# The second attention's gates on VectorE instead of GpSimd, and the last two outputs in place

## The chip, the cores and the metric

The kernel runs on one core of one Trainium2 chip. A core has five engines that work side by side: TensorE (PE) multiplies matrices into PSUM, VectorE (DVE) and ScalarE (ACT) work elementwise on SBUF and PSUM, GpSimd (POOL) works elementwise on SBUF, and SyncE (SP) issues DMAs here. The metric is the time of one execution on the device, in microseconds (us), lower being better.

## What is computed

The reference has two layers over x of 4 × 1024 tokens of width 128, all in fp32:

```python
xn = _layernorm(x)
s = _L0_attn_ref(xn, ...)            # 16 heads, window of 64 tokens, ALiBi
g = _silu(_L0_ffn_ref(xn, ...))      # 8 experts mixed into one weight per batch
x = x + s * g
xn = _layernorm(x)
s = _L1_attn_ref(xn, ...)            # below
g = _silu(_L1_ffn_ref(xn, ...))      # gated, then two square layers of 512, then back to 128
x = x + s * g
```

The second attention takes the first axis (4) as its sequence: each of the 1024 positions attends over its own 4 batch entries, with 16 heads of 8 elements. The part that the change touches is its gate on the position bias:

```python
g = jax.nn.sigmoid(g.reshape(B, H, T, 2, 4).sum(-1))
gate_a = g[..., 0:1]
gate_b = g[..., 1:2]
gate_a_1 = gate_a * (gate_b * grep_a - 1.0) + 2.0
attn = attn + gate_a_1 * position_bias[None]
probs = jax.nn.softmax(attn, axis=-1)
```

The kernel writes a sigmoid as 0.5 + 0.5 · tanh(half), so the gate becomes (tanh_a + 1) · (tanh_b · 0.25 · grep_a + 0.25 · grep_a − 0.5) + 2.

## The kernel before

**Stages.** x, xn and the second layer's gate g1 lie in SBUF as 128 partitions × 4 batches × 1024 tokens. The first layer and the second layer's feed-forward run over eight units of half a batch (512 tokens); the second attention runs over eight slices of 128 positions, each with all four batches. As the second attention of a slice needs nothing but its own 128 columns of the four batches, it starts while the first layer still runs (from about 340 us) and ends with the kernel. Slices 0 to 3 need the first halves of the batches, slices 4 to 7 (`late`) the second halves.

**Order.** ORDER is a list written out by hand. Each word is one step, and the steps emit their instructions engine by engine in just that order; each engine runs its own instructions in order, so an instruction that waits holds up all behind it on its engine. Words with a star belong to the second attention: for slice n, `*An` projects one batch (four times), `*Bn` takes the gates' tanh, `*bn` forms the products, `*Cn` the scores, `*En` the exponentials, `*Nn` the normalisation, `*Dn` the values (twice, two batch entries each), `*Gn` their total, `*Tn` turns back, `*Fn` projects out, `*Yn` writes the slice's output. `wn`, `hn`, `in` and `jn` are the quarters of unit n's feed-forward: the gated pair (two matrices of 128×512), the two square layers, and the way back. The list ends:

```python
*C6 h7 *E6 *F1 *A7 *B7 h7 *Y4 *F5 h7 *N6 *b7 *Y1 *C7 h7 *E7 *D6 *Y5 *N7 *T2 i7 *F2 *D7 *D6 *D7 *G6 i7
*Y2 i7 *F0 *T6 *G7 *F3 *F6 *Y3 *T7 *Y6 i7 *F7 j7 *Y0 *Y7 j7 y0 y1
```

**The steps that matter here.** `attend` holds the second attention. `products` (`*b`) multiplies each query by each key on VectorE (L631) and then, on GpSimd, forms the gate ga from the tanh values in six operations (L640 to L646), the last of which, gb, multiplies it with the position bias for all 4 × 4 pairs. `score` (`*C`) sums the products over a head's elements (L658, L660), adds gb (L661) and takes the maximum off (L664, L665). `norm` (L674 to L676) and `values` (L682 on VectorE, L689 on GpSimd) follow, `total` is L694. `gated_out` (`*Y`) adds the bias out of PSUM (L715), multiplies with g1 (L716), adds x on GpSimd (L717) and starts a DMA (L718).

For late slices `gated_out` writes only batches 0 to 2. The last batch's second half waits for the feed-forward of the last unit (`j7`, L590 on TensorE and L593 on ScalarE, in two halves), and is written by `last_batch` (`y0`, `y1`) in two pieces of 256 columns: xn times g1 (L732), plus x (L733), and a DMA (L734). Both `gated_out` and `last_batch` take a buffer `t2k` for it, of which there are three in rotation; so a step can't write its buffer before the DMA of the step three buffers earlier has read it.

**Banks.** PSUM banks are taken in the order of the table BANKS, one digit a request, from three banks M0 to M2: a request waits until the last reader of that bank's earlier content is done. In the feed-forward's gated pair the second bank of a pair is read by L569 on VectorE, the first by L568 on ScalarE; the square layers' banks are read by L578 on ScalarE, the projections' by L620 and L621.

Of the kernel before, what the change touches and what calls it, by code (L numbers as in the profile page):

```python
# [12 lines left out]
ALU = mybir.AluOpType  # L13
# [3 lines left out]
P = 128  # L17
B, S, D = 4, 1024, 128
H, HD = 16, 8
# [20 lines left out]
G = 2 * H  # L40
# [6 lines left out]
def constants():  # L47
# [67 lines left out]
BANKS = (  # L115
    "0120120120102102102102102121021012012012021021020120120120120201201201201201021012010210210212102102"
    "1021020120121210210210210210212121010201201212012021021021021210210210210210210210210210210201021021"
    "010210210210210210210210210210210210210210120120120120120120120101201202101012"
)


# [1 line left out]
def block_kernel(ctx: ExitStack, tc: tile.TileContext, a: dict, out: bass.AP):  # L123
    nc = tc.nc
    PE, DVE, ACT, POOL = nc.tensor, nc.vector, nc.scalar, nc.gpsimd
# [14 lines left out]
    def t2k():  # L140
        return tmp.tile([P, 512], F32, tag="t2k", name="t2k", bufs=3)
# [7 lines left out]
    g1 = main.tile([P, B, S], F32, tag="g1", name="g1")  # L149
# [12 lines left out]
    qga = const.tile([P, 2, H], F32, tag="qga", name="qga")  # L162
# [13 lines left out]
    def v(name, i=0, n=1):  # L176
        at = VEC[name][0] + i
        return vec[:, at:at + n]
# [5 lines left out]
    xn = main.tile([P, B, S], F32, tag="xn", name="xn")  # L184
# [103 lines left out]
    def program(exact):  # L288
# [8 lines left out]
        def big(shape=(P, 4, 4, P)):  # L297
            return ffn.tile(list(shape), F32, tag="big", name="big", bufs=6)
# [298 lines left out]
        def attend(sl, pool, late):  # L597
# [30 lines left out]
            def products():  # L628
                pd = st["pd"] = big((P, B, B, D))
                m = st["qkg"]  # L630
                DVE.tensor_tensor(  # L631
                    pd,
                    m[:, :, 0:D].unsqueeze(2).to_broadcast([P, B, B, D]),
                    m[:, :, D:2 * D].unsqueeze(1).to_broadcast([P, B, B, D]),
                    ALU.mult,
                )

                gate = st["gate"]
                ga = pool.tile([P, B, H], F32, tag="ga", name="ga")
                POOL.tensor_tensor(ga, gate[:, :, H:G], qga[:, 0:1, :].to_broadcast([P, B, H]), ALU.mult)  # L640
                POOL.tensor_tensor(ga, ga, qga[:, 1:2, :].to_broadcast([P, B, H]), ALU.add)
                POOL.tensor_scalar(gate[:, :, 0:H], gate[:, :, 0:H], 1.0, None, ALU.add)
                POOL.tensor_tensor(ga, ga, gate[:, :, 0:H], ALU.mult)
                POOL.tensor_scalar(ga, ga, 2.0, None, ALU.add)
                gb = st["gb"] = pool.tile([P, B, B, H], F32, tag="gb", name="gb")
                POOL.tensor_tensor(  # L646
                    gb,
                    ga.unsqueeze(2).to_broadcast([P, B, B, H]),
                    v("pb", 0, B * B * H).rearrange("p (t s h) -> p t s h", t=B, s=B),
                    ALU.mult,  # L650
                )
# [56 lines left out]
            def gated_out():  # L708
# [10 lines left out]

            steps_of = {  # L720
                "B": gates, "b": products, "C": score, "E": power, "N": norm, "G": total, "T": turn_back, "F": project_out, "Y": gated_out,
            }
            for letter, parts_of in (("A", project), ("D", values)):
# [3 lines left out]
        def last_batch(i):  # L727

            n = U // 2
            y = t2k()[:, 0:n]  # L730
            r = slice(U + i * n, U + i * n + n)
            DVE.tensor_tensor(y, xn[:, B - 1, r], g1[:, B - 1, r], ALU.mult)  # L732
            DVE.tensor_tensor(y, y, x[:, B - 1, r], ALU.add)  # L733
            nc.sync.dma_start(out=out[:, (B - 1) * S + r.start:(B - 1) * S + r.stop], in_=y)  # L734

# [103 lines left out]
        def scaled_w3():  # L839
# [10 lines left out]
            "z": second_gates, "Z": scaled_w3,  # L850
            "L": lambda i: load(*(("w1", "w2", "h1"), ("h2", "w3"), ("wa", "x"))[i]), "0": lambda n: idle(cst, P * n), 
            "y": last_batch,
            **{"*" + c: slices(c) for c in "ABbCENDGTFY"},
        }
        banks["next"] = iter(BANKS[BEGIN:])
        for word in ORDER.split():
            n = 2 if word[0] == "*" else 1
# [78 lines left out]
```

## Time and profile before

| | |
|---|---|
| median of 3 runs | 540.52 us (540.14 to 540.78) |
| the profiled execution | 540.1 us, of which the span 538.3 us |
| TensorE's granted clock | 0.99 of full speed over the span |
| the gates on GpSimd, L640 to L646, 8 times each | 4.2, 7.8, 7.5, 5.4, 4.4 and 8.4 us busy |
| VectorE's L661 idle before it for gb | 3.0 us in 4 places |
| products, L631, 128×2048 | 2.30 us each, 8 times |
| last two L732 and L733 | 0.47 and 0.42 us each |

How much each engine has to do in the stretches of the second attention (start and end, length, and busy time of PE, PEld, DVE, ACT and POOL, then clock, DMA share and GB/s):

```profile
340.00:375.00 35.00, 35.00 (x360) 18.20 (x360) 22.41 (x31) 28.16 (x36) 7.55 (x14) 1.00 0.01 1
395.00:420.00 25.00, 24.91 (x202) 13.19 (x205) 19.56 (x27) 18.82 (x22) 7.13 (x8) 1.00 0.01 2
440.00:475.00 35.00, 34.90 (x88) 15.87 (x87) 29.18 (x43) 23.78 (x34) 16.09 (x16) 1.00 0.00 0
475.00:490.00 15.00, 15.00 (x77) 10.32 (x76) 12.29 (x21) 8.85 (x16) 6.46 (x6) 1.00 0.00 1
490.00:530.00 40.00, 39.13 (x157) 22.57 (x156) 36.89 (x48) 17.65 (x25) 25.91 (x23) 1.00 0.12 36
```

TensorE is busy in all of them. VectorE is busy 22.4 of 35 us at the beginning of the second attention, and 36.9 of 40 at its end. A number before a line's bracket in later views is idle time of that engine ahead of the instruction, with what ended it. Numbers of lines are those of the kernel before.

### The profile page before, as it was taken

The numbers are of one execution on the slowest core, as the hardware profiler recorded it, in microseconds if no ns is written. First come the engines' busy times: TensorE is split into PE (matmuls) and PEld (weight loads), VectorE is DVE, ScalarE is ACT, GpSimd is POOL, SyncE is SP. The second block draws the span as 40 slices with busy tenths as digits, with TensorE's granted clock in tenths as the row PEclk, the third lists the DMA queues.
The fourth block names the chain that finished last, engine by engine and source line by source line (L and its number), as shares of the span: only waits on it lengthen the run. The fifth ranks groups of instructions, "written<-read, shape, count | busy, mean of one in ns | idle before, by whom it ended". The sixth has DMA issues, their size and how long they took to land.

```text
span 538.3 us, 10515 instructions
## 1 busy us (share of the span) xinstructions
PE 520.2 (97%) x4448; PEld 293.6 (55%) x4448; DVE 348.5 (65%) x657; ACT 369.1 (69%) x436; POOL 124.2 (23%) x149
## 2 busy tenths in 40 slices
PE   8599999999999999999999999999999999999994
PEld 4267554475465645555555674554564564455463
DVE  6899885466465443415745554665778577988993
ACT  3678673797859676694999637887995655765432
POOL 4013230110011010000020020211613253725762
PEclk9899999999999999999999999999999999999998
DMA  8925021110240011021301000000000000000103
GB/s 315 414 80 197 3 75 44 40 62 20 81 154 3 2 40 39 2 79 39 118 2 40 1 1 1 2 2 0 1 1 2 1 0 1 0 1 2 35 24 105
DMA packets 10727, 27.33 MB, mean 51 GB/s; under 512 B 1040, under 2 KB 5296, under 8 KB 9648
## 3 DMA queue, kind: packets, MB, share of 16 engines
q1 hardware_dynamic: 10240, 25.01, 13.3%
q10 hardware_dynamic: 432, 1.57, 0.8%
q8 instruction: 37, 0.61, 0.5%
q14 instruction: 18, 0.15, 0.1%
HBM read 24.48 MB, written 2.10 MB: 49 GB/s over the span
## 4 chain that ended last, share of the span: by engine, by line
PE 77%; DVE 12%; POOL 3%; ACT 3%; issue 2%; DMA 1%; DVEq 0%; POOLq 0%; ACTq 0%
PE ps_M L577 32%; PE ps_S L426 6%; PE ps_O L474 5%; PE ps_M L517 5%; PE ps_M L590 5%; PE ps_M L528 4%; PE ps_M L565 4%; PE ps_M L566 4%; PE ps_M L619 3%; DVE big L682 2%; DVE big L443 2%; PE ps_M L232 1%; DMA out<-t2k 1%; PE ps_M L273 1%; ACT big L777 1%
## 5 line engine op out<-in xcount | busy, mean ns | idle before, releaser
L577 PE MATMUL ps_M<-big,l1h 128*128 128x512 f32 x512 | 229.3, 595 | 0.9 <-ACT big L578 0.5
L577 PEld LDWEIGHTS ps_M<-big,l1h 128*128 128x128 f32 x512 | 94.9, 190 | 111.8 <-issue 105.9
L443 DVE TENSOR_TENSOR big<-ps_S,bias 128x2048 f32<-128x2048 f32 x32 | 73.2, 2287 | 32.4 <-PE ps_S L426 26.4
L578 ACT ACTIVATE big<-ps_M,vec 128x512 f32<-128x512 f32 x64 | 43.7, 687 | 60.5 <-PE ps_M L577 60.2
L777 ACT ACTIVATE big<-big 128x2048 f32<-128x2048 f32 x32 | 60.9, 1910 | 9.1 <-DVE big L443 8.8
L578 ACT ACT_TABLE_LOAD x41 | 52.6, 1283 | 7.6 <-PE ps_M L577 6.9
L538 POOL TENSOR_TENSOR g<-g,s 128x512 f32<-128x512 f32 x8 | 10.2, 1273 | 200.1 <-DVE s L508 130.7
L569 DVE SCALAR_TENSOR_TENSOR big<-ps_M,vec,t2k 128x512 f32<-128x512 f32 x32 | 24.0, 749 | 36.3 <-PE ps_M L566 19.9
L426 PE MATMUL ps_S<-qm,k 32*64 32x256 f32 (+1 forms) x768 | 37.4, 472 | 4.5 <-DVE big L443 4.3
L474 PEld LDWEIGHTS ps_O<-big,vb 128*32 128x32 f32 x2048 | 30.3, 112 | 11.1 <-issue 8.0
L568 ACT ACTIVATE t2k<-ps_M,vec 128x512 f32<-128x512 f32 x32 | 22.0, 686 | 19.4 <-PE ps_M L565 19.2
L474 PE MATMUL ps_O<-big,vb 128*32 128x64 f32 x2048 | 33.4, 223 | 1.0 <-issue 0.6
L565 PE MATMUL ps_M<-xn,l1w 128*128 128x512 f32 x64 | 33.4, 603 | 0.2
L566 PE MATMUL ps_M<-xn,l1w 128*128 128x512 f32 x64 | 32.8, 594 | 0.8 <-ACT t2k L568 0.8
L517 PE MATMUL ps_M<-xn,mw 128*128 128x512 f32 x64 | 33.3, 609 | 0.0
L528 PEld LDWEIGHTS ps_M<-mw,big 128*128 128x128 f32 x256 | 30.1, 192 | 4.1 <-issue 3.0
L590 PEld LDWEIGHTS ps_M<-l1w,big 128*128 128x128 f32 x256 | 30.2, 192 | 4.0 <-issue 3.6
L352 DVE SCALAR_TENSOR_TENSOR mw<-tw,gr,mw 128x512 f32<-128x512 f32 x42 | 31.1, 746 | 0.5
L528 PE MATMUL ps_M<-mw,big 128*128 128x128 f32 x256 | 31.1, 276 | 0.0
L590 PE MATMUL ps_M<-l1w,big 128*128 128x128 f32 x256 | 30.9, 276 | 0.0
L214 POOL TENSOR_SCALAR rstd<-mv 128x4 f32<-128x4 f32 x16 | 8.4, 527 | 97.3 <-DVE mv L212 90.8
L689 POOL TENSOR_TENSOR big<-big 128x512 f32<-128x512 f32 x16 | 22.2, 1387 | 34.5 <-DVE big L682 34.5
(164 smaller groups left out, 734.7 us busy)
## 6 DMA issues: line engine op xcount, KB each, us to landing
tw<-in_tw SPq DMA_DIRECT2D x24, 512.0 KB, 4.0
big<-in_tw SPq DMA_DIRECT2D x4, 1024.0 KB, 9.2
l1h<-in_l1h SPq DMA_DIRECT2D x2, 1024.0 KB, 8.6
bias<-in_bias ACTq DMA_DIRECT2D x1, 1024.0 KB, 8.7
x<-in_x SPq DMA_DIRECT2D x1, 1024.0 KB, 5.2
out<-t2k SPq DMA_DIRECT2D x4, 256.0 KB, 2.9
l1w<-in_l1w SPq DMA_DIRECT2D x3, 256.0 KB, 9.8
out<-t2k SPq DMA_DIRECT2D x4, 192.0 KB, 2.2
```

The source lines that it names most:

```text
L352: DVE.scalar_tensor_tensor(m, more[e // 2][:, e % 2, :], gr[:, e:e + 1], base if e == 0 else m, ALU.mult, ALU.add)
L426: PE.matmul(sp[rows, j, :, q0:q0 + n], lhsT=k[r, key:key + W], rhs=qm[r, :, t * P + q0:t * P + q0 + n], start=True, stop=True,)
L443: DVE.tensor_tensor(pr, sp, bias, ALU.add)
L474: PE.matmul(op[32 * j:32 * j + 32, part, qs], lhsT=vb[:, col:col + 32], rhs=pr[:, j, g, qs], start=(odd + i + g == 0), stop=(odd + i + g = ...
L517: PE.matmul(hp, lhsT=m1[:, c * P:(c + 1) * P], rhs=xn[:, b, cx], start=True, stop=True)
L528: PE.matmul(op[:, i, :], lhsT=hid[:, c, i * P:(i + 1) * P], rhs=m2[:, c * D:(c + 1) * D], start=(c + i == 0), stop=(c + i == FC + 2))
L565: PE.matmul(p1, lhsT=wt["w1"][:, c * P:(c + 1) * P], rhs=xn[:, b, cx], start=True, stop=True)
L566: PE.matmul(p2, lhsT=wt["w2"][:, c * P:(c + 1) * P], rhs=xn[:, b, cx], start=True, stop=True)
L577: PE.matmul(hp, lhsT=wt[name][:, i, c * P:(c + 1) * P], rhs=hid[:, i, :], start=(i == 0), stop=(i == FC - 1))
L578: ACT.activation(new[:, c, :], hp, AF.Gelu, scale=v(name + "s", c))
L590: PE.matmul(op[:, k, :], lhsT=hid[:, i, at0:at0 + P], rhs=wt["w3"][:, i, :], start=(i + k == 0), stop=(i + k == FC + n - 2))
L777: ACT.activation(pr, pr, AF.Exp)
```

## The change

The six operations of the gates move from GpSimd to VectorE; two of them, adding 1 to tanh_a and multiplying it in, become one fused operation, which leaves the tile `gate` as it was. They stay at their place in the program, after the products of the same slice. The two pieces of `last_batch` write into xn itself instead of a `t2k` buffer, and are sent from there. In BANKS eleven of the last twelve digits are others: from `*T2` on the requests take other ones of the three banks (`*F2` alone keeps M1).

```diff
-    "010210210210210210210210210210210210210210210120120120120120120120101201202101012"
+    "010210210210210210210210210210210210210210210120120120120120120120101021020212120"
...
                 gate = st["gate"]
                 ga = pool.tile([P, B, H], F32, tag="ga", name="ga")
-                POOL.tensor_tensor(ga, gate[:, :, H:G], qga[:, 0:1, :].to_broadcast([P, B, H]), ALU.mult)
-                POOL.tensor_tensor(ga, ga, qga[:, 1:2, :].to_broadcast([P, B, H]), ALU.add)
-                POOL.tensor_scalar(gate[:, :, 0:H], gate[:, :, 0:H], 1.0, None, ALU.add)
-                POOL.tensor_tensor(ga, ga, gate[:, :, 0:H], ALU.mult)
-                POOL.tensor_scalar(ga, ga, 2.0, None, ALU.add)
+                DVE.tensor_tensor(ga, gate[:, :, H:G], qga[:, 0:1, :].to_broadcast([P, B, H]), ALU.mult)
+                DVE.tensor_tensor(ga, ga, qga[:, 1:2, :].to_broadcast([P, B, H]), ALU.add)
+                DVE.scalar_tensor_tensor(ga, gate[:, :, 0:H], 1.0, ga, ALU.add, ALU.mult)
                 gb = st["gb"] = pool.tile([P, B, B, H], F32, tag="gb", name="gb")
-                POOL.tensor_tensor(
+                DVE.tensor_scalar(ga, ga, 2.0, None, ALU.add)
+                DVE.tensor_tensor(
                     gb,
                     ga.unsqueeze(2).to_broadcast([P, B, B, H]),
                     v("pb", 0, B * B * H).rearrange("p (t s h) -> p t s h", t=B, s=B),
...
             n = U // 2
-            y = t2k()[:, 0:n]
             r = slice(U + i * n, U + i * n + n)
-            DVE.tensor_tensor(y, xn[:, B - 1, r], g1[:, B - 1, r], ALU.mult)
+            y = xn[:, B - 1, r]
+            DVE.tensor_tensor(y, y, g1[:, B - 1, r], ALU.mult)
             DVE.tensor_tensor(y, y, x[:, B - 1, r], ALU.add)
             nc.sync.dma_start(out=out[:, (B - 1) * S + r.start:(B - 1) * S + r.stop], in_=y)
```

More of the change, by code (lines that the diff above doesn't have):

```diff
@@ L117 @@
     "1021020120121210210210210210212121010201201212012021021021021210210210210210210210210210210201021021"
-    "010210210210210210210210210210210210210210120120120120120120120101201202101012"
+    "010210210210210210210210210210210210210210120120120120120120120101021020212120"
 )
```

## The prediction

> **What bounds the kernel now.** I read four views in this order: the page's busy times and chain, the chain from 390 us on, the timeline around the places where that chain leaves TensorE, and the groups of instructions with shapes kept apart, for prices. First the page:
>
> ```profile
> PE 520.2 (97%) x4448; PEld 293.6 (55%) x4448; DVE 348.5 (65%) x657; ACT 369.1 (69%) x436; POOL 124.2 (23%) x149
> PE 77%; DVE 12%; POOL 3%; ACT 3%; issue 2%; DMA 1%; DVEq 0%; POOLq 0%; ACTq 0%
> ```
>
> TensorE has work nearly throughout, so a change elsewhere counts only where TensorE waits for it, or after its last instruction. The 23% left to others sit mostly in the second half. The chain from 390 us on (start, length, engine, tile, line) shows where:
>
> ```profile
> 457.68 2.46 POOL gate L642
> 463.09 0.44 DVE vb L661
> 465.25 2.21 DVE big L631
> 473.67 0.75 DVE big L569
> 474.47 1.13 PE ps_M L565 x2
> ...
> 494.05 0.86 POOL gb L646
> 494.94 0.43 DVE vb L661
> ...
> 499.63 2.32 DVE big L631
> ...
> 528.76 4.38 DMA out<-t2k
> 533.14 0.03 issue
> ```
>
> From 457.6 to 474.4 the chain is VectorE with GpSimd's gates inside it, and ends in a TensorE that waits for L569. From 489 to 523 it is VectorE almost without a gap, and at the end the last output waits for a DMA of the output two before it. The timeline of these places says how much slack there is (start, length; idle before and its releaser in brackets):
>
> ```profile
> 463.09 0.43 DVE L661 TENSOR_TENSOR vb<-vb,gb 128x256 f32<-128x256 f32 x1 [0.54 <-POOL gb L646]
> 474.47 0.30 PEld L565 LDWEIGHTS ps_M<-xn,l1w 128*128 128x128 f32 x2 [0.93 <-DVE big L569]
> ...
> 531.47 0.38 ACT L593 ACTIVATE g<-ps_M 128x256 f32<-128x256 f32 x1 [1.40 <-PE ps_M L590]
> 533.26 0.43 DVE L732 TENSOR_TENSOR t2k<-xn,g 128x256 f32<-128x256 f32 x1 [2.14 <-DMA out<-t2k]
> ```
>
> VectorE stops for the gates only where a slice's products and their sums are shorter than GpSimd's six operations; it waits 3.0 us in all, in four places (1.40, 0.54, 0.54, 0.54). TensorE at 474.47 starts 0.06 after L569's end: any delay of VectorE arrives there whole.
>
> [...] L642 on GpSimd takes 0.37 us alone and 2.48 beside the 2.28 us of L631, and L658 of a slice takes 1.94 us alone (at 353.97) but 2.27 at 467.48 where a gate operation holds it. [...]
>
> **The change part by part.** Prices from the groups by shape:
>
> ```profile
> L508 DVE TENSOR_TENSOR s<-ps_M,inv 128x64 f32<-128x64 f32 x16 | 3.4, 215 | 0.0
> L332 DVE TENSOR_TENSOR shares<-tb,gr 128x32 f32<-128x32 f32 x4 | 0.7, 186 | 0.1
> L661 DVE TENSOR_TENSOR vb<-vb,gb 128x256 f32<-128x256 f32 x4 | 1.7, 426 | 1.3 <-POOL gb L646 1.1
> L327 DVE SCALAR_TENSOR_TENSOR gr<-ps_M,vec 128x8 f32<-128x8 f32 x4 | 0.6, 161 | 1.2 <-PE ps_M L325 1.1
> L835 DVE TENSOR_SCALAR wa<-wa 128x128 f32<-128x128 f32 x1 | 0.2, 217 | 0.0
> ```
>
> Added per slice: two tensor_tensor of 64 elements, 0.22 each (between L332 and L661, and L508's 0.215); one fused operation of 64, 0.23 (L327's 0.161 at 8 elements, L352's 0.746 at 512); one tensor_scalar of 64, 0.19 (below L835's 128); gb, 0.43. Sum 1.29, plus 0.03 between dependent VectorE instructions (L664 ends at 464.13, L665 starts at 464.16) five times: 1.44 us. Eight slices: 11.5 us. Bounds: 1.25 (0.19 for each small one, no gaps) and 1.7 (0.25 each and gb at 0.55). Removed: GpSimd's 37.7 us (4.2+7.8+7.5+5.4+4.4+8.4). None is itself TensorE's wait; its worth is the four stops and the collisions.
>
> Instructions behind the new ones on VectorE are those behind L631 in each slice. Their order, and that of every other engine and of the DMA queue, is unchanged. New is only that VectorE itself now waits for the gate's tanh (L626); in all eight slices that ends before or within 0.2 us of L631, so this costs nothing.
>
> - Slices 0 to 3 (344 to 440 us). In slice 0, L443 starts 1.7 us later (347.7) and delays ScalarE's copies; ScalarE still has 0.35 us before L578 at 357.03 and 0.41 before L518 at 360.01. Of its 0.76 us about 0.3 reach TensorE at 361.0. In slice 1 VectorE is 1.44 late, but ScalarE idles 2.00 before L578 at 369.78 and VectorE 2.26 at 372.50. In slice 2, 1.44 replaces a wait of 1.40: nothing. In slice 3, VectorE waits 1.24 for GpSimd's rstd just behind the gates; what is left is gone at the 1.26 of idle time before L674 (441.59). Together +0.3 (bounds 0 and 0.8).
> - Slices 4 and 5. +1.44 − 0.54 = +0.90; then +1.44 − 0.32 (L658 at 2.27 back to 1.95) − 0.08 (the gap before L661) = +1.04. L569 ends 1.94 later and TensorE starts 1.94 later at 474.47; no TensorE idle time follows until 496 in which to regain it. With slices 0 to 3: +2.24.
> - Slices 6 and 7. VectorE carries 2.24 + (1.44 − 0.13 − 0.54) + (1.44 − 0.12 − 0.35) = +3.98 out of L661 of slice 7 (0.13 and 0.12: L631's 2.41 and 2.40 back to 2.28; 0.35: L658 at 2.30). L660's 1.57 beside L717 I leave in: L717, freed of the gates before it, meets another two-input operation instead.
> - The tail. VectorE is busy from there to 523 without waiting, so the last square's last part, L577 at 523.37, comes to wait for L715, which ends at 522.78, 0.53 before that start allowing for 0.06 of semaphore. TensorE's last work moves by 3.98 − 0.53 = +3.45. The later banks in the table swap which of two instructions waits for L715; either way the later one does.
> - The outputs in place. L732 and L733 keep their prices (two and two). The last L732 no longer waits for a t2k buffer: it can start at 531.47 + 0.38 + 0.05 = 531.90 in place of 533.26, −1.36. The first pair waited for ScalarE anyway. Were the pace set by that DMA, this would be worth all of 1.36, and it is.
>
> Sum: +3.45 − 1.36 = +2.1 us. The profiled execution took 540.1 us around a span of 538.3, so 542.2; the median of the runs is 540.52, 0.4 above it, so I say 542.6. About 0.2% (1.1 us) is what a measurement here can tell from no change.
>
> **Rivals.**
> - *VectorE pays more (544.7).* The gates cost 1.6 us, slices 0 to 3 leak 0.8 because ScalarE has less slack than I read, and the collisions (0.32+0.08+0.13+0.12+0.35) move to other operations of GpSimd: 4 × 1.6 − 1.08 + 0.8 − 0.53 − 1.36 = +4.2. For it: GpSimd's sums at L689 hit L682 as much as the gates did. Against it: between 452 and 475 GpSimd has nothing else to do.
> - *No difference (540.9).* Small operations overlap more than dependent rows show, so a slice costs about 1.0: 4 × 1.0 − 2.08 + 0.3 − 0.53 − 1.36 = +0.3. For it: L502 starts 0.08 before L501's listed end. Against: those two don't depend on each other; the gates' five do.
> - *Faster (539.2).* The wait for the DMA is gone (−1.36) and VectorE's late gates don't reach TensorE: the mechanism would be a TensorE that arrives late at 474.47 and 523.37 for a reason of its own. It decides if TensorE's end moves by less than 1.36, that is for a slice's gates at or below 0.9 us (4g − 2.08 + 0.3 − 0.53 < 1.36, g for a slice and 2.08 for the stops and collisions above). For it: GpSimd is 3% of the chain, 16 us, all of which leaves. Against: 0.93 of idle time at L565 shows TensorE early, and five instructions cannot fit in 0.9 at 0.16 for the smallest.
> - *That it doesn't do what it says*: the wait lists of the changed program show VectorE's L661 without GpSimd and the last L732 without a DMA, so I give it nothing.
>
> **How the numbers follow.** Slower as worked out 0.68; more 0.12; no difference 0.12; faster 0.08. The likeliest one's own range is 541.5 (a slice at 1.25, no leak) to 543.7 (a slice at 1.7, leak 0.3). For 8 in 10 I take 540.8 to 544.3: it takes in most of no difference, and leaves out faster and the upper half of the dearest case. Slower by over 0.2% means over 541.6: 0.68 × 0.93 + 0.12 = 0.75; within: 0.17; faster: 0.08.
>
> **What would show it.** Right: five VectorE instructions of 0.19 to 0.43 us behind each L631; no GpSimd between 452 and 475 us; L565 behind slice 5 near 476.7, still waiting for L569; TensorE's last sums (L590) 3 to 4 us later; the last L732 released by ScalarE within 0.1 us; L661 never released by GpSimd. Wrong: L565 released by something else, or VectorE with idle time in the last 40 us; or slice sums below 1.2 us.

## The result, and the profile after

The changed kernel takes 541.75 us (median; 540.27 to 542.53) against 540.07 us (539.41 to 540.78) for the kernel before on the same chip: a ratio of 1.0026, 95% interval 1.0019 to 1.0032. It is slower, by 1.68 us. Its profiled execution took 541.8 us with a span of 540.0. In the views and line numbers below, from `products` on the changed kernel's numbers are one less than before: L640 to L645 are the gates, L657 to L660 the sums up to the addition of gb, L731 to L733 the last outputs.

The page of the changed kernel, busy time and chain of waits by engine:

```profile
PE 520.4 (96%) x4448; PEld 293.3 (54%) x4448; DVE 357.2 (66%) x697; ACT 368.9 (68%) x436; POOL 85.8 (16%) x101
PE 83%; DVE 12%; ACT 2%; issue 1%; ACTq 0%; DVEq 0%
```

GpSimd's 3% and the DMA's 1% have left the chain, and GpSimd has lost 38.4 us of work. VectorE gained 8.7. Both waits that the change aims at are gone, and the kernel is slower all the same. The timeline of VectorE in slice 4 (start, length, instruction; in brackets idle time before it and its releaser):

```profile
457.93 2.28 DVE L631 TENSOR_TENSOR big<-qkg 128x2048 f32<-128x2048 f32 x1
460.13 0.22 DVE L640 TENSOR_TENSOR ga<-gate,qga 128x64 f32<-128x64 f32 x1
460.38 0.22 DVE L641 TENSOR_TENSOR ga<-ga,qga 128x64 f32<-128x64 f32 x1
460.64 0.22 DVE L642 SCALAR_TENSOR_TENSOR ga<-gate,ga 128x64 f32<-128x64 f32 x1
460.90 0.20 DVE L644 TENSOR_SCALAR ga<-ga 128x64 f32<-128x64 f32 x1
461.13 0.42 DVE L645 TENSOR_TENSOR gb<-ga,vec 128x256 f32<-128x256 f32 x1
461.47 1.95 DVE L657 TENSOR_TENSOR big<-big 128x1024 f32<-128x1024 f32 x2
```

Read the starts and not the lengths. L640 starts 0.08 us before the listed end of L631, on which it doesn't depend, and L657 starts 0.08 before the listed end of L645. From L640's start to L657's it is 1.34 us. Before, from L631's start to the start of the sums was 2.31 us:

```profile
457.62 2.28 DVE L631 TENSOR_TENSOR big<-qkg 128x2048 f32<-128x2048 f32 x1
459.93 1.95 DVE L658 TENSOR_TENSOR big<-big 128x1024 f32<-128x1024 f32 x2
```

Now it is 3.54. So a slice's gates cost 1.23 us of VectorE.

The timeline of TensorE at the two places where VectorE delays it, and of VectorE at the end:

```profile
476.33 1.12 PE L565 MATMUL ps_M<-xn,l1w 128*128 128x512 f32 x2 [1.64 <-DVE big L569]
...
523.22 0.63 PE L699 MATMUL ps_M<-cst,big 128*128 128x128 f32 x4 [1.18 <-DVE big L693]
...
531.80 0.64 DVE L715 TENSOR_TENSOR t2k<-xn,g 128x384 f32<-128x384 f32 x1 [0.39 <-DMA out<-t2k]
532.85 0.95 DVE L731 TENSOR_TENSOR xn<-xn,g 128x256 f32<-128x256 f32 x1 [0.41 <-ACT g L593]
...
534.64 0.42 DVE L731 TENSOR_TENSOR xn<-xn,g 128x256 f32<-128x256 f32 x1 [0.38 <-ACT g L593]
535.10 0.42 DVE L732 TENSOR_TENSOR xn<-xn,x 128x256 f32<-128x256 f32 x1
```

TensorE waits 1.64 us for L569 behind slice 5 (0.93 before) and 1.18 at L699. Before, L699 was L700, and waited 0.34:

```profile
520.53 0.63 PE L700 MATMUL ps_M<-cst,big 128*128 128x128 f32 x4 [0.34 <-DVE t2k L715]
```

The last product follows ScalarE at once instead of waiting for a DMA.

To compare executions I cut each one in three: up to the start of the first projection product L619 at about 340 us (the change touches nothing before it), from there to the end of the last addition, and from there to the end of the span. The first part varies from 340.30 to 341.07 between traces, the last, which I call the landing of the last output, from 3.4 to 5.4. The middle part repeats to 0.03 us where a kernel was profiled twice. All times below are in us. The three right-hand columns come from the timelines; "after L619" counts from the start of the first L619:

| kernel | median of its runs | L565 behind slice 5, after L619 | last addition's end, after L619 | from there to the span's end |
|---|---|---|---|---|
| before | 540.07 | 133.78 | 193.45 | 4.16 |
| changed | 541.75 | 135.26 | 194.45 | 4.48 |
| changed, again | 541.65 | 135.27 | 194.46 | 5.01 |
| gates alone | 542.18 | 135.25 | 195.79 | 3.97 |
| in place, gates of slices 0–3, new table | 538.91 | 133.72 | 191.59 | 4.66 |
| in place, gates of slices 4–7, new table | 541.81 | 135.30 | 194.46 | 4.06 |
| changed, old table | 541.01 | 135.25 | 194.97 | 3.58 |
| in place alone | 538.23 | 133.76 | 192.06 | 3.44 |
| in place alone, again | 537.97 | 133.76 | 192.05 | 3.46 |
| in place, new table | 538.53 | 133.76 | 191.63 | 4.09 |
| in place, +1 on ScalarE | 537.66 | 133.24 | 191.67 | 3.38 |
| the same, again | 537.85 | 133.22 | 191.64 | 3.46 |
| gates twice in slices 4–7 | 549.81 | 138.19 | 202.30 | 5.37 |
| gates twice in slices 4, 5 | 545.32 | 138.18 | 199.06 | 4.69 |

Of the 1.68 us, the middle part holds 1.00.

### The profile page after: what moved, and what is told of

It is laid out like the page before. It is cut to its first block, busy times and chain, and to the rows that moved or that the text cites. A ratio compares the mean times of both kernels' runs of the same rounds, so it can differ in the third digit from the quotient of the medians.

```text
span 540.0 us, 10488 instructions
## 1 busy us (share of the span) xinstructions
PE 520.4 (96%) x4448; PEld 293.3 (54%) x4448; DVE 357.2 (66%) x697; ACT 368.9 (68%) x436; POOL 85.8 (16%) x101
## 3 DMA queue, kind: packets, MB, share of 16 engines
q10 hardware_dynamic: 432, 1.57, 0.8%
## 4 chain that ended last, share of the span: by engine, by line
PE 83%; DVE 12%; ACT 2%; issue 1%; ACTq 0%; DVEq 0%
PE ps_M L577 33%; PE ps_S L426 6%; PE ps_O L474 5%; PE ps_M L590 5%; PE ps_M L528 5%; PE ps_M L517 5%; PE ps_M L565 5%; PE ps_M L566 5%; PE ps_M L619 4%; DVE big L631 2%; DVE big L443 2%; DVE big L657 2%; PE ps_M L273 1%; PE ps_M L232 1%; DVE big L681 1%
## 5 line engine op out<-in xcount | busy, mean ns | idle before, releaser
L577 PE MATMUL ps_M<-big,l1h 128*128 128x512 f32 x512 | 229.4, 595 | 0.9 <-ACT big L578 0.5
L577 PEld LDWEIGHTS ps_M<-big,l1h 128*128 128x128 f32 x512 | 94.9, 190 | 111.8 <-issue 105.7
L569 DVE SCALAR_TENSOR_TENSOR big<-ps_M,vec,t2k 128x512 f32<-128x512 f32 x32 | 24.0, 749 | 35.2 <-PE ps_M L566 20.0
L426 PE MATMUL ps_S<-qm,k 32*64 32x256 f32 (+1 forms) x768 | 37.4, 472 | 4.7 <-DVE big L443 4.3
L565 PE MATMUL ps_M<-xn,l1w 128*128 128x512 f32 x64 | 33.4, 604 | 1.7 <-DVE big L569 1.6
L590 PEld LDWEIGHTS ps_M<-l1w,big 128*128 128x128 f32 x256 | 30.2, 192 | 4.0 <-issue 3.6
L590 PE MATMUL ps_M<-l1w,big 128*128 128x128 f32 x256 | 30.9, 276 | 0.0
L426 PEld LDWEIGHTS ps_S<-qm,k 32*64 32x64 f32 x768 | 18.7, 133 | 20.8 <-issue 7.0
```

What stands on the lines that cost most here:

```text
L426: PE.matmul(sp[rows, j, :, q0:q0 + n], lhsT=k[r, key:key + W], rhs=qm[r, :, t * P + q0:t * P + q0 + n], start=True, stop=True,)
L565: PE.matmul(p1, lhsT=wt["w1"][:, c * P:(c + 1) * P], rhs=xn[:, b, cx], start=True, stop=True)
L577: PE.matmul(hp, lhsT=wt[name][:, i, c * P:(c + 1) * P], rhs=hid[:, i, :], start=(i == 0), stop=(i == FC - 1))
L590: PE.matmul(op[:, k, :], lhsT=hid[:, i, at0:at0 + P], rhs=wt["w3"][:, i, :], start=(i + k == 0), stop=(i + k == FC + n - 2))
```

## The experiments

My theory was that of the prediction: the gates of slices 4 to 7 lie on the path and reach TensorE's end, those of slices 0 to 3 don't, and the outputs in place give 1.36 us back. The rivals: a part of the loss comes from slices 0 to 3, from the bank table or from moved collisions.

**1. Outputs in place alone** (gates on GpSimd, bank table of before).

```diff
-            y = t2k()[:, 0:n]
-            DVE.tensor_tensor(y, xn[:, B - 1, r], g1[:, B - 1, r], ALU.mult)
+            y = xn[:, B - 1, r]
+            DVE.tensor_tensor(y, y, g1[:, B - 1, r], ALU.mult)
```

> Only the two last outputs are written in place; the gates stay on GpSimd. If the wait of the last L732 for the DMA two outputs before it set the end, it gains its 1.36 us: about 538.7 against 540.07 before. If the end is set by the DMAs' landing anyway, it stays at 540.1.

Measured: 538.23 us, ratio 0.9973 (0.9962 to 0.9984). The timeline of VectorE at the end of this kernel:

```profile
531.48 0.43 DVE L732 TENSOR_TENSOR xn<-xn,g 128x256 f32<-128x256 f32 x1 [0.76 <-ACT g L593]
```

The wait for the DMA is gone, the middle part is 1.39 us shorter, and the last output lands 0.7 us sooner after the last addition. This part of the change is a gain of 1.8 us.

**2. Gates alone** (VectorE's gates and the new bank table; the outputs through t2k as before).

```diff
-            y = xn[:, B - 1, r]
+            y = t2k()[:, 0:n]
```

> Only the gates move to VectorE (with the changed banks); the two last outputs keep their t2k buffers. VectorE's late output before them is landed at about 536.1 to 536.5 in the trace of after (532.0 plus 3.8 to 4.4), so the last L732 starts 1.5 to 1.9 us later than in after: 543.3 to 543.6. If writing in place is worth nothing once TensorE ends later, it is equal to after, 541.75.

Measured: 542.18 us, ratio 1.0040 (1.0027 to 1.0053), only 0.43 above the changed kernel. The chain of waits of this kernel shows the old wait again:

```profile
531.60 3.83 DMA out<-t2k
535.43 0.03 issue
535.46 0.05 DVEq L731
535.51 0.04 issue
535.55 0.44 DVE t2k L731
```

In the middle part the wait costs 1.34 us (195.79 against 194.45), close to the prediction's 1.36 and less than the 1.5 to 1.9 expected here. Its last output then lands in 3.97 us, while the changed kernel's needs 4.48 and 5.01. So 0.5 to 1.0 us of what the outputs in place save ahead of the last addition is lost after it. That did not happen in experiment 1, so something else in the changed kernel does it; experiments 6 and 9 look for it.

**3. In place, VectorE's gates in slices 0 to 3 only** and **4. in slices 4 to 7 only**, both with the new bank table.

```diff
+                if not late:
                     DVE.tensor_tensor(ga, gate[:, :, H:G], ...
...
+                else:
+                    POOL.tensor_tensor(ga, gate[:, :, H:G], ...
```

(the second of them with `if late`.)

> Outputs in place, gates on VectorE only in slices 0 to 3 and on GpSimd in slices 4 to 7. If the early slices are covered, as the trace of after has it (TensorE 0.38 us later at 341 and 0.32 at 457), it equals the kernel with the outputs in place alone, 538.7. If they leak the 0.3 us of the prediction, 539.0; if they leak 0.8, 539.5.

> Outputs in place, gates on VectorE only in slices 4 to 7 and on GpSimd in slices 0 to 3. If the whole loss lies in the late slices, it equals after, 541.75. If half of it lies in the early ones, about 540.3.

Measured: 538.91 us, ratio 0.9978 (0.9970 to 0.9987), and 541.81 us, ratio 1.0038 (1.0026 to 1.0051). The late gates alone give the changed kernel's time, and its middle part to 0.01 us. The early ones change the middle part by −0.04 (191.59 against 191.63 for experiment 9, which differs from it in nothing else). Slices 0 to 3 leak nothing in the middle part; the whole price lies in slices 4 to 7. Experiment 4 against 9, which differ in nothing but the late gates, gives it again: 2.83 (194.46 against 191.63).

**5. The changed kernel again**, beside experiments 6 to 8 on one chip.

> The changed kernel once more, so that its time stands beside the other versions of this call on one chip, and to see what its runs vary by. Theory: its time is set by VectorE's late gates and by the landing of the last output, which alone varies by about 1.3 us between executions (3.4 to 4.7 us from the last add's end to the end of the span in the traces so far): 541.75 within 0.5, again with single runs from about 540.3 to 542.5. Rival: the first set of runs met something of its own (a start 0.38 us later in the trace), and the time is now 541.4 or below.

Measured: 541.65 us (539.91 to 542.14), ratio 1.0024 (1.0015 to 1.0033). The middle part is that of the first trace (194.46), and the start is 0.64 us earlier: the late start of the first trace was not what made the kernel slower. The runs of one kernel vary by at least two things in the traces, the start and the landing of the last output.

**6. The changed kernel with the old bank table.**

```diff
-    "...120120120120120120120101021020212120"
+    "...120120120120120120120101201202101012"
```

> The changed kernel with the bank table of the kernel before. Theory: which of the two last instructions waits for a bank is all that the table changes, and the later one waits for L714 either way: the time of the changed kernel within 0.3 us, TensorE's last sums (L590) within 0.3 us of 530.45. Rival: the new table carries part of the loss, then this is 0.5 us or more faster than the changed kernel.

Measured: 541.01 us, ratio 1.0016 (1.0009 to 1.0022), 0.64 under the changed kernel measured beside it, though the two intervals overlap. TensorE comes *later* with the old table, as its timeline shows against the L699 shown above:

```profile
523.78 0.63 PE L699 MATMUL ps_M<-cst,big 128*128 128x128 f32 x4 [1.77 <-DVE t2k L714]
```

With the old table L699 waits for L714, with the new one only for L693, which VectorE runs just ahead of L714. That makes the new table 0.52 us better in the middle part (194.45 against 194.97). But with the old table the landing is 3.58 us in place of 4.48 and 5.01. The theory failed here: in these traces the table matters twice, with opposite signs.

**7. The five gates twice in slices 4 to 7.**

```diff
+                if late:
+                    DVE.tensor_tensor(ga, gate[:, :, H:G], qga[:, 0:1, :].to_broadcast([P, B, H]), ALU.mult)
...
```

> The changed kernel with the five gate operations of slices 4 to 7 issued twice on VectorE (the second time they write the same values again). Theory: VectorE's time in these slices reaches TensorE's end whole, once the stops for GpSimd and the slack of 0.53 are spent: a second set costs 4 x 1.23 = 4.9 us, so 546.7, L565 behind slice 5 2.5 us later (near 478.8) and L590 4.9 later (near 535.4). If the price were 1.44 a slice, as predicted, 5.8 and 547.5. Rival: part of the loss is something else (the bank table, the collisions, the later tanh): then a second set costs clearly less than 4 us, 545.5 or below.

Measured: 549.81 us, ratio 1.0168 (1.0150 to 1.0186), 8.2 above the changed kernel and far from both theories. Two things came out. First, the price. The timeline of VectorE in slice 4 of this kernel:

```profile
459.39 0.22 DVE L640 TENSOR_TENSOR ga<-gate,qga 128x64 f32<-128x64 f32 x1
...
460.39 0.42 DVE L645 TENSOR_TENSOR gb<-ga,vec 128x256 f32<-128x256 f32 x1
460.85 0.22 DVE L652 TENSOR_TENSOR ga<-gate,qga 128x64 f32<-128x64 f32 x1
...
462.20 1.95 DVE L668 TENSOR_TENSOR big<-big 128x1024 f32<-128x1024 f32 x2
```

L652 must wait until L645 has read ga, so it starts 0.04 after its end. From the first set to the second it is 1.46 us, and L565 behind slice 5 comes 2.93 us later than in the changed kernel: 2 × 1.46. Where each instruction waits for the one before, the five cost what I had predicted (1.44); the set that stands between instructions it does not depend on costs 0.23 less.

Second, TensorE's clock. The same stretch of time in the changed kernel and in this one (start and end, length, busy time of PE and its instructions, granted clock, DMA share, GB/s); the changed kernel first:

```profile
475.00:480.00 5.00, 3.67 (x9) 1.00 0.01 3
480.00:485.00 5.00, 5.00 (x28) 1.00 0.00 0
```

With the gates twice:

```profile
475.00:476.00 1.00, 0.05 (x1) 1.00 0.00 0
476.00:477.00 1.00, 0.00 (x0) 1.00 0.00 0
477.00:478.00 1.00, 0.00 (x0) 1.00 0.00 0
478.00:479.00 1.00, 0.48 (x1) 1.00 0.02 8
479.00:480.00 1.00, 1.00 (x3) 0.78 0.00 0
480.00:481.00 1.00, 1.00 (x2) 0.50 0.03 8
481.00:482.00 1.00, 1.00 (x3) 0.50 0.00 0
482.00:483.00 1.00, 1.00 (x3) 0.51 0.00 0
483.00:484.00 1.00, 1.00 (x4) 1.00 0.00 0
```

TensorE's wait before L565 has become 3.47 us, and about a microsecond after it resumes, its clock falls to half for 3.4 us: 0.22 + 0.50 + 0.50 + 0.49 = 1.71 us of work lost. The same happens once more at 520.5 us, after a wait of 1.89 us. So this kernel is no clean measure of the gates' price; experiment 12 separates the two.

**8. In place, gates on GpSimd, the addition of 1 on ScalarE.**

```diff
                 ACT.activation(gate, st["qkg"][:, :, 2 * D:N_QKG], AF.Tanh, scale=0.5)
+                ACT.activation(gate[:, :, 0:H], gate[:, :, 0:H], AF.Copy, bias=1.0)
...
-                POOL.tensor_scalar(gate[:, :, 0:H], gate[:, :, 0:H], 1.0, None, ALU.add)
```

> The outputs in place and the gates on GpSimd as before, but the addition of one to half of the tanh moved from GpSimd (L642) to ScalarE, directly behind the tanh. GpSimd has five operations left, and the one that is held by the products (L631) for 2.5 us is then the product L643. Theory: the stops of 0.54 us before L661 in slices 4, 5 and 7 go, VectorE is about 1.1 us earlier at L569 and 1.1 to 1.6 us earlier in the last slices, and this comes out in the end: 536.6 to 537.2, beside 538.2 for the outputs in place alone. Rival: ScalarE's 0.25 us more a slice delays the tanh of the next slices and the copies, or what VectorE gains in the last slices is lost to the copies of the last project: 538.2 or above.

Measured: 537.66 us, ratio 0.9953 (0.9939 to 0.9966), less of a gain than expected. The stops of 0.54 us before L661 lie in slices 3, 4 and 6, not in 4, 5 and 7 as the expectation has it, and they are gone; the stop of slice 2 is 1.00 us instead of 1.40, and ScalarE pays 0.26 us for each addition. Against experiment 1 TensorE is 0.34 us earlier behind slice 2 (L577 at 74.88 after L619 for 75.22) and 0.52 earlier behind slice 5 (L565), where it no longer waits. But most of a stop comes back in the sums, which now run beside other operations of GpSimd: L660 in slice 4 takes 0.94 us for 0.62, so that L661 there gains 0.12 more and not 0.54, and in slice 7 the two of L658 take 3.33 for 2.30, of which L660 gives 0.96 back. So of the 1.1 us and more that VectorE was to gain, the middle part gets 0.39 (191.67 against 192.06).

**9. In place alone with the new bank table**, **10. in place alone again**, **11. the addition on ScalarE again**, on one chip. Experiment 9 is the kernel of experiment 1 with the new table, 10 is that of 1, and 11 that of 8.

> The outputs in place, the gates on GpSimd, and the changed kernel's bank table: one part more than the outputs in place alone. Theory: the new table brings TensorE's end 0.2 to 0.5 us forward but lets the last output of the sums (L717) go out closer to the two final outputs, and their landing takes 4.1 to 5.0 us from the last add's end to the span's end in place of 3.4 to 3.6: 538.7 to 538.9, beside 538.2 for the old table. Rival: the 0.6 us between the changed kernel with its own table and with the old one is scatter between calls and runs, the table is worth nothing: 538.2.

> The outputs in place alone once more, on one chip with the new bank table and with the addition of one on ScalarE. Theory: 538.2 within 0.4, the last add 3.4 to 3.6 us ahead of the span's end. Rival: the first 538.23 of seven runs was low, and this is 538.8, like the early gates on VectorE, so that the new bank table costs nothing.

> The outputs in place and the addition of one on ScalarE once more, beside the outputs in place alone. Theory: the stops for the gates in slices 4, 5 and 7 are gone, TensorE no longer waits behind slice 5, and this is worth the 0.4 to 0.5 us that TensorE waited there: 537.7, 0.5 under the outputs in place alone. Rival: the difference of 0.57 was between two calls; then the two agree within 0.2.

Measured: 538.53 us, ratio 0.9974 (0.9962 to 0.9987); 537.97, 0.9965 (0.9955 to 0.9975); 537.85, 0.9962 (0.9948 to 0.9976). The new table again shortens the middle part (by 0.42) and lengthens the landing (4.09 against 3.46). With it L700, which waited 0.34 us before, starts without a wait:

```profile
519.85 0.66 PE L700 MATMUL ps_M<-cst,big 128*128 128x128 f32 x4
```

In all traces of kernels with the outputs in place and no doubled gates, the landing is 3.38 to 3.58 with the old table and 4.06 to 5.01 with the new one. By the medians the new table costs 0.56 us here and 0.64 in experiments 5 and 6; by each pair of intervals alone it could still be nothing. How the table lengthens the landing is not shown. What the timelines show is that the last addition follows the last addition of the sums on GpSimd (L716, or L717) by 2.4 us with the old table and by 1.8 to 2.1 with the new one, so that the last two transfers start closer to the one ahead of them. That is at most 0.6 us of a difference of up to 1.6.

The gain of the addition on ScalarE over the outputs in place alone is 0.4 us in the middle part in both pairs of traces. In the medians it was 0.57 and then 0.12: in device time it is not settled.

**12. The gates twice in slices 4 and 5 only.**

```diff
-                if late:
+                if sl in (4, 5):
                     DVE.tensor_tensor(ga, gate[:, :, H:G], ...
```

> The changed kernel with the five gate operations issued twice in slices 4 and 5 alone. Theory: the second set costs its time, 2 x 1.23 = 2.46, and the longer wait of TensorE behind slice 5 (3.5 us in place of 1.6) makes the granted clock fall to 0.50 for about 3.4 us, 1.7 us of TensorE's work lost: 541.7 + 2.5 + 1.7 = 545.9, with the low clock behind L565 and none at 520 to 525. Rival: the excess of 3.3 us with four second sets comes from the operations (dearer in the last slices) and not from the clock: then two sets here cost 2.5, 544.1.

Measured: 545.32 us, ratio 1.0100 (1.0084 to 1.0115). Its middle part is 4.61 us longer than the changed kernel's. The granted clock is 0.50 from 479.87 to 483.28 and full from 520 to 525, so one fall, of 1.71 us as before. 2 × 1.46 + 1.71 = 4.63. The rival, which left the clock out, falls for this trace. It is the slowest of four executions; the two fastest took 544.94 and 544.99 us at a mean clock of 0.991 instead of 0.985, 0.4 over 541.65 + 2 × 1.46, so the clock need not have fallen in each of them.

For the gates twice in all four slices the same sum gives 4 × 1.46 + 2 × 1.71 = 9.26, and the middle part grew by 7.84. The missing 1.4 us lie in the second fall. In experiment 7, L693 (there L704) ends up 7.60 us later than in the changed kernel, which is 4 × 1.46 + 1.71, and L699 (there L710), which waited 1.18 us for it in the changed kernel, starts without a wait, 7.88 later. So most of the second fall went where TensorE would have waited for VectorE.

## Why the prediction came out as it did

The sum of the middle part was predicted as +2.1 us and measured as +1.00; the landing, which it left out, added 0.3 to 0.9 in the two traces. The sign is that of the prediction, and so is the mechanism, VectorE's late gates on the path; the time is 0.85 under the forecast, within its own range. That the measured +1.68 comes so near +2.1 is in part luck: the middle part was over-priced by 1.1, and a landing that the sum left out made up for some of it. Step by step, with the starts of the traces taken out:

- *Price of a slice, 1.44:* mis-sized, 1.23 measured. The five durations were right: 0.22, 0.22, 0.22, 0.20, 0.42, where I had 0.22, 0.22, 0.23, 0.19, 0.43. The tensor_tensor ones are as long as those of the same width before (0.215 for 64 elements, 0.426 for 256; GpSimd took 0.32 at best for one of 64). The five gaps were the error: at the two ends of the set the neighbours overlap by 0.08 each instead of standing 0.03 apart. Over four slices that is 4 × 0.21 = 0.84, most of the 1.1 by which the middle part was missed; the leak is nearly all of the rest.
- *Leak of slices 0 to 3, +0.3:* −0.04. Behind slices 0 and 1 TensorE starts at the same times as before (L565 69.30 after L619 in both); in slice 2 the 1.23 us are less than the stop of 1.40 that they replace, and L577 behind it comes 0.07 earlier (75.16 for 75.23).
- *Slices 4 and 5, +1.94 at L565:* +1.48 (135.26 against 133.78). With 1.23 for 1.44 the same step gives 1.52.
- *Slices 6 and 7, +3.98 at L661, leak included:* +2.89 (L661 166.52 after L619 before, L660 169.41 now). Without the leak and with the right price it is 2.84. The collision moved as foreseen. The sums of slice 7, before and then now:

```profile
503.20 2.30 DVE L658 TENSOR_TENSOR big<-big 128x1024 f32<-128x1024 f32 x2
505.54 1.57 DVE L660 TENSOR_TENSOR vb<-big 128x256 f32<-128x256 f32 x1
507.21 0.43 DVE L661 TENSOR_TENSOR vb<-vb,gb 128x256 f32<-128x256 f32 x1
...
506.89 2.89 DVE L657 TENSOR_TENSOR big<-big 128x1024 f32<-128x1024 f32 x2
509.82 0.63 DVE L659 TENSOR_TENSOR vb<-big 128x256 f32<-128x256 f32 x1
510.48 0.43 DVE L660 TENSOR_TENSOR vb<-vb,gb 128x256 f32<-128x256 f32 x1
```

GpSimd's L716 now runs beside L657 (507.12 to 509.24 us), which takes 2.89 us for 1.95 in slice 4, as L717 had run beside L660 (1.57 for 0.62 in slice 4). The traces show these lengths and that the instructions run side by side; why the one is longer beside the other they do not show.
- *The tail, −0.53 of slack:* the size came out (+2.37 at L590 for +2.89 at L660), the reason was wrong. It was not L577 that came to wait for L715, but L700 two steps before it. With the old table there is no slack: from experiment 1 to experiment 6 the gates cost 2.91 in the middle part, all of what VectorE carries, for L700 was already waiting 0.34 us for L715 before the change. It is the new table that gives 0.52, by taking L714 out of L699's wait. I had said that the table makes no difference because the later instruction waits either way; that is the step that failed in kind.
- *In place, −1.36:* −1.39 in experiment 1, −1.34 between experiment 2 and the changed kernel. That it is also worth 0.7 of landing with the old table, and loses that with the new one, was not in the sum, which stopped at the last addition.

Taken one after another, from the kernel before over experiments 1, 9 and 3 to the changed kernel, the parts of the middle are −1.39 (in place), −0.43 (table), −0.04 (slices 0 to 3) and +2.86 (slices 4 to 7), +1.00 in all. Such a chain adds up by construction; that the parts don't depend much on each other is shown by the gates (2.83 for the late ones alone, 2.91 for all of them with the old table) and the outputs in place (1.39 and 1.34). In device time, by the medians: −1.8 for the outputs in place, about +0.6 for the table, and +2.9 for the late gates.

Of the signs named in advance, most came: no GpSimd between 452 and 475 us, L565 at 476.33 still waiting for L569, L660 never released by GpSimd, the last L731 released by ScalarE. L590 came 2.75 us later (2.37 without the later start) and not 3 to 4. By its words one sign of being wrong came too, VectorE idle in the last 40 us: 0.34 and 0.39 us for output DMAs from 529 us on, behind L699, where it held TensorE no more.

Of the rivals, *pays more* is refuted by the 1.23 us of the timeline and by experiment 3. *No difference* had the right observation, that small operations overlap, but took it for the middle of the set, where they stand 0.03 to 0.04 us apart, instead of its ends, where they overlap by 0.08. *Faster* needed 0.9 us a slice; VectorE's gates are far above that. (The prediction's reason against it was loose: five times 0.16 is 0.8; only with gb's 0.43 is the sum 1.07.) The version that beats both kernels keeps the gates on GpSimd and takes only the outputs in place with the old table: 538.23 and 537.97 us, 0.3 to 0.35% under the kernel before. The addition on ScalarE may take a few tenths off that.

## What to carry to other kernels

A wait for a slow engine is worth only its length: GpSimd's 3% of the chain were 16 us of presence but 3.0 us of stops, and filling the stops with 1.23 us a slice of the engine on the path cost more than they did: 4.92 us in slices 4 to 7, against 2.08 of stops and collisions there. Price an inserted group from start to start, with gaps only between the instructions that depend on each other (here 0.03 to 0.04 us, where independent ones overlapped by 0.08), and carry the sum past the last instruction to the landing of the last transfer. Test each part of a change alone: here a gain of 1.8 us was hidden under a loss of about 2.9.

## What was not expected of the hardware

TensorE's granted clock falls to 0.50 of full speed after waits hardly longer than those of the changed kernel. Six waits of the second attention, and the clock behind each (times in us):

| kernel | TensorE's wait | it resumes at | granted clock |
|---|---|---|---|
| changed | 1.64 before L565 | 476.33 | 1.00 from 475 to 485 |
| changed, again | 1.64 before L565 | 475.70 | 1.00 from 475 to 485 |
| changed, old table | 1.77 before L699 | 523.78 | 1.00 from 520 to 535 |
| gates twice in slices 4–7 | 3.47 before L565 | 478.52 | 0.50 from 479.57 to 482.98 |
| the same kernel | 1.89 before L716 | 519.87 | 0.50 from 520.53 to 523.94 |
| gates twice in slices 4, 5 | 3.47 before L565 | 478.63 | 0.50 from 479.87 to 483.28 |

Each of these three falls lasts 3.41 us, in which 1.71 us of work are lost, and begins 0.66 to 1.24 us after TensorE has resumed. In the traces of the kernel before and of the changed kernel the clock also falls near the start, at 21.85 and 20.99 us, for 6.83 us each: there TensorE waits 1.65 and 1.66 us before L325 and then 4.31 and 4.32 before L426, and the fall comes 1.9 and 0.8 us into the second wait.

In the table a wait of 1.77 us draws no fall and one of 1.89 does. Whether the length of one wait decides it is not shown, and what ends a fall is not either. A little more waiting than in the changed kernel may thus cost 1.7 us at once.
